# Layer 1's second convolution as a two-phase filter along the columns

## The chip, the cores and the metric

The kernel runs on one core of a Trainium2 chip. The time is the device time of one execution in microseconds. A core has TensorE (PE) for matmuls, with its weight loads shown apart as PEld, VectorE (DVE), ScalarE (ACT), GpSimd (POOL) and SyncE (SP); each has a queue of its own. SP and POOL also start the DMAs of this kernel.

## The reference, cut to what matters

An input of 16 images x 16 channels x 256 x 256 in float32 passes a spectral layer (layer 0) and then layer 1, the one that the change touches:

```python
def _L1_conv_ref(x, W1, b1, Wred, bred, Wspan, bspan, W2, b2, Weca):
    ...
    f = mish(conv2d(xs, W1, b1))
    top, bot = (f[:, :, :H2], f[:, :, H2:])
    ker = conv2d(jax.nn.relu(conv2d(bot, Wred, bred)), Wspan, bspan)
    ...
    top_inv = (patches * ker[:, None]).sum(axis=2)
    ...
    shuffled = shuffled.reshape(B, 4 * C, H, W)
    out = mish(conv2d(shuffled, W2, b2))
    pooled = out.mean(axis=(2, 3))
    ...
    gate = jax.nn.sigmoid(Weca[0] * yp[:, :-2] + Weca[1] * yp[:, 1:-1] + Weca[2] * yp[:, 2:])
    return x * gate[:, :, None, None]
```

The second convolution has 64 input channels, 16 output channels and 3 x 3 taps. Only the mean of its Mish over an image is used. So each output pixel has to be computed, but none is stored.

## The kernel before

The program has four stages: three for layer 0 (`layer0_forward`, `layer0_mix`, `layer0_back`), which end at about 3620 us of the profile, and `layer1` after them. Layer 1 works on one image after the other. An image is cut into nine units (`blocks`): eight of 32 rows x 8 channels, and a ninth with what is left, which has half the work.

A unit passes through these pieces, all methods of `Unit`:

- `lower`: two pairs of matmuls (first convolution of the lower half of the image, names "c", L1027) and four Mish on ScalarE into `bot` (L1046).
- `reduce`: four small matmuls ("pr", L1054), two Relu on ScalarE into `r` (L1063), and the stores of `bot` into the DRAM buffer `cf` (`store_bot`, L1147), issued by GpSimd.
- `upper(0)` and `upper(1)`: a pair of matmuls each (again "c", L1027), and eight Mish each on ScalarE into `wide` (L1075), 32 partitions at a time.
- `spread`: eight copies on GpSimd inside `wide` (L1087, L1088), two for each of four features.
- `involution(0)` to `involution(3)`: two matmuls each ("pd", L1095), and for each of them three VectorE operations (L1103, L1106) into `top`. After the last, `store_top` (L1117, L1124, L1129) writes `top` to `cf`, with GpSimd issuing four or five DMAs, and 16 for a ninth unit.

The second convolution of an image follows one image behind, in eight steps, one for each of the first eight units of the next image. `conv2_rows` loads 17 row pairs of `cf` into one of two buffers `rows2`, on SP, one step ahead. In such a row pair 128 partitions hold 2 rows x 64 channels, and the 256 columns stand in two halves: the odd columns first, then the even ones, with a column of zeros at either end. `conv2` then computes the two column phases one after the other (`q`). Each phase is three column shifts x two row blocks x four groups of 32 output columns of TensorE. The four groups write four quarters of one PSUM bank (`ps2`, one buffer). ScalarE applies Mish to the bank and sums it (L1178).

[...]two buffers of two banks for "c" (`ps1`), three banks for "pd" and "pr" (`psd`), and one for `c2ps` (`ps2`).

When an image's second convolution is done, `gate` computes the 16 gate values in the ninth step and then works on the output in four parts: one in the ninth step, and one in each of the next three. A part is eight scalings on GpSimd (L1216) and two DMAs that it issues (L1225). The loads for the parts (L1193) are in SP's queue.

The order of all these pieces on TensorE, ScalarE, VectorE and GpSimd is written out by hand (`manual_schedule`): an engine takes its instructions in the order in which the loop issues them. A step of the loop (`now` is the current unit, `nxt` the one after it):

```python
            if nxt:
                nxt.lower()
            if now:
                now.involution(0)
            next(second, None)
            ...
            next(last, None)
            next(second, None)
            if now:
                now.involution(3)
```

Between these stand, in order, `nxt.reduce()`, `now.involution(1)`, `nxt.upper(0)`, `now.involution(2)`, `nxt.upper(1)` and `nxt.spread()`. `second` is the step of `conv2`, `last` the gate.

Of the kernel before, what the change touches and what calls it, by code (L numbers as in the profile page):

```python
# [10 lines left out]
F32 = mybir.dt.float32  # L11
I32 = mybir.dt.int32
AF = mybir.ActivationFunctionType
ALU = mybir.AluOpType
# [7 lines left out]
P = 128  # L22
# [34 lines left out]
def load(nc, pool, src, shape, name):  # L57
    t = pool.tile(shape, F32, tag=name, name=name)
    nc.sync.dma_start(out=t, in_=src)
    return t  # L60
# [870 lines left out]
def layer1(ctx, tc, d, zn, cf, mr, nb):  # L931
# [7 lines left out]
    nc = tc.nc  # L939
    H = N // 2  # L940
    wp = ctx.enter_context(tc.tile_pool(name="l1w", bufs=1))
    zp = ctx.enter_context(tc.tile_pool(name="l1z", bufs=4))
    fp = ctx.enter_context(tc.tile_pool(name="l1f", bufs=2))
    rp = ctx.enter_context(tc.tile_pool(name="l1r", bufs=3))
# [3 lines left out]
    psd = ctx.enter_context(tc.tile_pool(name="psd", bufs=3, space=PSUM))  # L948
    ps2 = ctx.enter_context(tc.tile_pool(name="ps2", bufs=1, space=PSUM))
# [6 lines left out]
    wr = load(nc, wp, d["wr"], [P, 32], "wr")  # L956
    dw = load(nc, wp, d["dw"], [P, P], "dw")
    dwt = load(nc, wp, d["dwt"], [P, P], "dwt")
    c2 = load(nc, wp, d["c2"], [P, 2, 3, 32], "c2")
    pm = load(nc, wp, d["pm"], [P, 3, C], "pm")  # L960
    weca = wp.tile([P, 3], F32, name="weca")
    nc.sync.dma_start(out=weca, in_=d["weca"].to_broadcast([P, 3]))
# [8 lines left out]
    b2 = load(nc, wp, d["b2"], [P, 1], "b2")  # L971
# [20 lines left out]
    for t in rows2:  # L992
        for x in (0, N + 1):
            nc.gpsimd.memset(t[:, :, x : x + 1], 0.0)

    def load_rows(b, half, j, h):

        z = zp.tile([P, 8, N + 2], F32, tag="z", name="z")
        flat = z.rearrange("p c x -> p (c x)")
        row = C * (N + 2)  # L1000
        if j < 4:

            m = 8 * (N + 2) - 2
            src = zn[b, H * half + 30 * j, 8 * h, 0:1]
            for dx in range(3):
                win = bass.AP(src.tensor, src.offset + dx, [[row, 32], [1, m]])
                nc.sync.dma_start(out=flat[32 * dx : 32 * dx + 32, :m], in_=win)
            for i in range(2):
                win = bass.AP(src.tensor, src.offset + (32 + i) * row, [[1, 3], [1, m]])
                nc.sync.dma_start(out=flat[96 + 3 * i : 99 + 3 * i, :m], in_=win)  # L1010
            return z
        m = 4 * (N + 2) - 2
        src = zn[b, H * half + 120, 0, 0:1]
        for dx in range(3):
            for c in range(4):
                p = 40 * dx + 10 * c
                win = bass.AP(src.tensor, src.offset + dx + 4 * (N + 2) * c, [[row, 10], [1, m]])
                nc.sync.dma_start(out=flat[p : p + 10, :m], in_=win)
        return z
# [132 lines left out]
    def conv2_rows(b, s):  # L1152
        t = rows2[(8 * b + s) % 2]
        flat = cf[b % 4].rearrange("(t y) f c x -> (y f c) t x", y=2)
        nc.sync.dma_start(out=t[:, :, 1 : N + 1], in_=flat[:, 16 * s : 16 * s + 17])

    def conv2(b, s, acc):


        t = rows2[(8 * b + s) % 2]  # L1160

        begin = ((H + 1, 1, H + 2), (0, H + 1, 1))
        for q in range(2):
            ps = ps2.tile([P, 4, H], F32, tag="c2", name="c2ps")
            for blk in range(2):
                for dx in range(3):
                    x = begin[q][dx]
                    for j in range(4):
                        nc.tensor.matmul(  # L1169
                            ps[32 * j : 32 * j + 32],  # L1170
                            lhsT=c2[:, blk, dx, :],
                            rhs=t[:, 4 * j + blk : 4 * j + blk + 4, x : x + H],
                            start=(blk, dx) == (0, 0),
                            stop=(blk, dx) == (1, 2),
                        )
            e = rp.tile([P, 4, H], F32, tag="e2", name="e2", bufs=2)
            k = 2 * s + q
            nc.scalar.activation(e, ps, AF.Mish, bias=b2, accum_out=acc[:, k : k + 1])  # L1178
            yield

    def gate(b, acc):

# [52 lines left out]
    def begin_unit(i):  # L1235
        if i < len(order):
            b, s = order[i]
            units[i] = Unit(b, i, *blocks[s])

    E = mybir.EngineType  # L1240
    with tc.manual_schedule(engines={E.PE, E.Activation, E.DVE, E.Pool}):
        begin_unit(0)
        begin_unit(1)
        u = units[0]
        u.lower()
        u.reduce()
        u.upper(0)
        u.upper(1)
        u.spread()
        acc, last = None, iter(())  # L1250
        for i in range(9 * nb + 12):
            b, s = divmod(i, 9)
            now, nxt = units.pop(i, None), units.get(i + 1)
            begin_unit(i + 2)
            second = iter(())
            if s == 8 and b < nb:
                conv2_rows(b, 0)
            if s == 8 and b and b <= nb:
                last = gate(b - 1, acc)
                next(last)  # L1260
            if s < 8 and b and b <= nb:
                if s == 0:
                    acc = sm.tile([P, 16], F32, tag="acc", name="acc")
                if s < 7:
                    conv2_rows(b - 1, s + 1)
                second = conv2(b - 1, s, acc)
# [6 lines that stand above are left out]
                nxt.reduce()  # L1273
            if s == 8:
                next(last, None)
            if now:
                now.involution(1)
            if nxt:
                nxt.upper(0)
            if now:  # L1280
                now.involution(2)
            if s == 8:
                next(last, None)
            if nxt:
                nxt.upper(1)
                nxt.spread()
            next(last, None)
            next(second, None)
            if now:
                now.involution(3)  # L1290

# [156 lines left out]
@with_exitstack  # L1450
def forward(ctx, tc, d):
    nb = d["x"].shape[0]
    dram = ctx.enter_context(tc.tile_pool(name="dram", bufs=1, space=DRAM))
    keep = ctx.enter_context(tc.tile_pool(name="keep", bufs=1))
    al = dram.tile([NF, 2, 64, nb, N], F32, name="al")
    bd = dram.tile([nb, P, P], F32, name="bd")
    hd = dram.tile([2, 2, 64, nb, C, N], F32, name="hd")
    tabs = (
        dram.tile([P, 2, C, N], F32, name="td"),
        dram.tile([NF, P, 384], F32, name="avd"),  # L1460
        dram.tile([P, 2, C, N], F32, name="ed"),
    )
    zn = dram.tile([nb, N + 2, C, N + 2], F32, name="zn")
    cf = dram.tile([4, N + 2, 4, C, N], F32, name="cf")
    mr = keep.tile([P, nb, G, 2], F32, name="mr")
    layer0_forward(tc, d, al, bd, tabs)
    layer0_mix(tc, d, al, hd, tabs)
    layer0_back(tc, d, hd, bd, zn, mr, tabs[2])
    layer1(tc, d, zn, cf, mr, nb)
# [25 lines left out]
```

## Time and profile before

| What | Value |
|---|---|
| Median of 3 runs | 7388.45 us (7382.54 to 7390.2) |
| Profiled execution | 7392.98 us |
| Its span | 7391.2 us |
| Mean granted TensorE clock | 0.968 |
| c2ps matmuls (L1169) | 12288, busy 1395.3 us |
| c matmuls (L1027), full units | 2048, busy 1014.2 us |
| pd matmuls (L1095), full units | 2048, busy 1012.5 us |
| Mish into wide (L1075) | 2176, busy 1477.4 us, 679 ns each |
| Copies in wide (L1087, L1088), full units | 1024, 1035 and 1041 ns each |
| Mish of c2ps (L1178) | 256, 687 ns each, then 193 ns for the sum |
| Scalings of the gate (L1216) | 512, 555 ns each |

A float32 matmul is two instructions in the trace, so that 128 steps x 2 phases x 24 matmuls make 12288 rows. The four column groups of c2ps run side by side: the duration of one row (about 600 ns) is not what it takes of TensorE's time. "Busy" counts overlapping rows once. The chain of waits follows the work that ended last backwards; where it stays on one engine, this engine is the bound there. In the timeline, an arrow names what ended the idle time before a row.

### The profile page before, as it was taken

What the parts mean: (1) busy time and instruction counts of PE and PEld (TensorE: products, weight loads), DVE (VectorE), ACT (ScalarE), POOL (GpSimd) and SP (SyncE); (2) the same over time, 40 slices, a digit from 0 to 9 for tenths busy, and PEclk for the clock granted to TensorE, in tenths of its full rate; (3) what the DMA queues carried; (4) which work ended last, traced back from release to release, by engine and by line L of the source; (5) the groups of instructions that cost most, each with busy time, mean ns of one, the idle gap of its engine ahead of it and who ended that gap; (6) DMA issues with size and microseconds to landing.
All of it is one profiled execution on the core that took longest, in us unless ns stands there. A gap on an engine that the chain in (4) does not pass through costs nothing.

```text
span 7391.2 us, 147380 instructions
## 1 busy us (share of the span) xinstructions
PE 6831.1 (92%) x57640; PEld 3890.3 (53%) x57640; DVE 4961.8 (67%) x9441; ACT 3806.5 (51%) x5915; POOL 3475.6 (47%) x4636
## 2 busy tenths in 40 slices
PE   7889999799999999899789999999999999999996
PEld 5778888566666666677423333333333333333332
DVE  8999975366666666788676656665666666666662
ACT  2223333366666666222366656666666666656662
POOL 2334444322222222566554655555665565655554
PEclk9899999899999999999889999999999999999999
DMA  3444444333333332899767888888888888888886
GB/s 99 111 117 119 118 124 117 109 95 97 98 98 98 98 98 83 305 326 326 249 181 221 259 242 253 252 258 254 253 253 251 256 249 267 256 247 251 256 265 205
DMA packets 716089, 1443.59 MB, mean 195 GB/s; under 512 B 98954, under 2 KB 525254, under 8 KB 673638
## 3 DMA queue, kind: packets, MB, share of 16 engines
q1 hardware_dynamic: 567206, 959.76, 43.4%
q0 software_dynamic: 148192, 474.40, 20.6%
q8 instruction: 460, 7.54, 0.4%
q14 instruction: 231, 1.89, 0.1%
HBM read 877.12 MB, written 556.47 MB: 194 GB/s over the span
## 4 chain that ended last, share of the span: by engine, by line
PE 64%; DVE 7%; ACT 4%; issue 3%; DMA 2%; POOL 0%; SPq 0%; DVEq 0%; ACTq 0%; POOLq 0%
PE c2ps L1169 17%; PE c L1027 12%; PE pd L1095 12%; PE ph L698 5%; PE ps L641 5%; PE pg L663 4%; ACT wide L1075 3%; DVE alb L600 2%; PE pr L1054 2%; PE py L858 2%; PE py L859 2%; PE pt L679 1%; DVE zb L890 1%; DVE st L875 1%; DMA rows<-cf 1%
## 5 line engine op out<-in xcount | busy, mean ns | idle before, releaser
L1075 ACT ACTIVATE wide<-c,b 32x512 f32<-32x512 f32 x2176 | 1477.4, 679 | 354.6 <-PE c L1027 302.8
L1103 DVE TENSOR_TENSOR t<-pd,r 64x512 f32<-64x512 f32 x1088 | 744.3, 684 | 1295.9 <-PE pd L1095 1270.3
L1106 DVE TENSOR_TENSOR top<-pd,t 32x512 f32<-32x512 f32 x2176 | 1504.2, 691 | 52.6
L1169 PE MATMUL c2ps<-rows,c 128*32 128x512 f32 x12288 | 1395.3, 601 | 26.6 <-ACT e L1178 13.7
L1087 POOL COPY wide<-wide 32x1031 f32<-32x1031 f32 (+1 forms) x576 | 568.9, 988 | 1239.0 <-ACT wide L1075 1211.7
L1027 PE MATMUL c<-z,w 102*128 102x512 f32 x2048 | 1014.2, 628 | 138.5 <-ACT wide L1075 115.4
L1095 PE MATMUL pd<-wide,dw 128*128 128x512 f32 x2048 | 1012.5, 616 | 6.4 <-ACT r L1063 2.5
L1169 PEld LDWEIGHTS c2ps<-rows,c 128*32 128x32 f32 x12288 | 393.0, 109 | 993.6 <-issue 885.3
L718 POOL DMA_DIRECT2D hd<-h x512 | 323.5, 639 | 1227.6 <-DVE h L711 1203.5
L1027 PEld LDWEIGHTS c<-z,w 102*128 102x128 f32 x2048 | 401.2, 198 | 675.9 <-issue 486.0
L1095 PEld LDWEIGHTS pd<-wide,dw 128*128 128x128 f32 x2048 | 376.8, 194 | 614.3 <-issue 449.0
L1178 ACT ACTIVATE e<-c2ps,b 128x512 f32<-128x512 f32 x256 | 175.9, 687 | 845.6 <-PE c2ps L1169 842.9
L1088 POOL COPY wide<-wide 32x1031 f32<-32x1031 f32 (+1 forms) x576 | 572.2, 993 | 35.8
L313 PE MATMUL px<-wxn,u 128*64 128x256 f32 x4224 | 557.8, 385 | 2.2 <-ACT o L320 2.1
L641 PE MATMUL ps<-tt,lt 128*64 128x256 f32 x4224 | 495.5, 384 | 38.9 <-DVE lt L627 35.9
L698 PE MATMUL ph<-ix,yt 64*128 64x256 f32 x4128 | 502.5, 391 | 5.4 <-issue 4.7
L313 PEld LDWEIGHTS px<-wxn,u 128*64 128x64 f32 x4224 | 400.7, 136 | 127.0 <-ACT o L320 5.1
L698 PEld LDWEIGHTS ph<-ix,yt 64*128 64x128 f32 x4128 | 392.7, 190 | 91.7 <-issue 44.6
L1046 ACT ACTIVATE bot<-c,b 128x512 f32<-128x512 f32 x544 | 344.1, 684 | 175.7 <-PE c L1027 168.2
L207 PE MATMUL pu<-fy,eo 128*128 128x128 f32 x2048 | 425.5, 291 | 6.0 <-DVE u L224 4.4
L320 ACT ACTIVATE o<-px,rsc 128x512 f32<-128x512 f32 (+1 forms) x272 | 186.0, 686 | 472.2 <-PE px L313 441.1
L871 POOL TENSOR_TENSOR x<-x,o 128x512 f32<-128x512 f32 x256 | 324.0, 1266 | 216.7 <-DVE o L870 215.3
(203 smaller groups left out, 10818.5 us busy)
## 6 DMA issues: line engine op xcount, KB each, us to landing
rows<-cf SPq DMA_DIRECT2D x128, 2176.0 KB
z<-zn SPq DMA_DIRECT2D x768, 257.8 KB
cf<-top POOLq DMA_DIRECT2D x512, 240.0 KB, 7.1
cf<-bot POOLq DMA_DIRECT2D x96, 840.0 KB, 11.6
alc<-al SPq DMA_DIRECT2D x264, 256.0 KB
zn<-zb SPq DMA_DIRECT2D x128, 516.0 KB
o<-zn SPq DMA_DIRECT2D x128, 516.0 KB
z<-in_x SPq DMA_DIRECT2D x64, 1024.0 KB
```

The costliest lines, as they stand in the source:

```text
L207: nc.tensor.matmul(pu[:, xh, e].rearrange("p v m -> p (v m)"), lhsT=lhs, rhs=fy[:, e], start=True, stop=True,)
L313: nc.tensor.matmul(ps[64 * k : 64 * k + 64, :, h], lhsT=u[:, h, part, g0 + j + k].rearrange("p f c -> p (f c)"), rhs=wxn[:, h, part], star ...
L641: nc.tensor.matmul(ps[64 * h : 64 * h + 64, v], lhsT=lt[:, h, k, 1 - v : 3 - v].rearrange("p l f c -> p (l f c)"), rhs=tt[:, h, k], start= ...
L698: nc.tensor.matmul(ph[q][:, e], lhsT=yt[lanes, i].rearrange("p t k -> p (t k)"), rhs=ix[lanes, i], start=n == 0, stop=n == 3,)
L1027: nc.tensor.matmul(ps[:, a], lhsT=w, rhs=z[:k, c : c + 2, 0:N], start=True, stop=True)
L1075: nc.scalar.activation(self.feat[64 - 32 * q : 96 - 32 * q, f, self.groups[g], :H], ps[q][32 * f : 32 * f + 32], AF.Mish, bias=b1[0][32 * ...
L1087: nc.gpsimd.tensor_copy(flat[0:32, f, 1:m], flat[64:96, f, 0 : m - 1])
L1088: nc.gpsimd.tensor_copy(flat[96:128, f, 0 : m - 1], flat[32:64, f, 1:m])
L1095: nc.tensor.matmul(ps, lhsT=dwt if self.tail else dw, rhs=self.feat[:, f, cs, :H], start=True, stop=True,)
L1103: nc.vector.tensor_tensor(t[64:128], ps[:64], self.r[:, cs], ALU.mult)
L1106: nc.vector.tensor_tensor(self.top[32 * f : 32 * f + 32, cs, q], ps[lanes], t[lanes], ALU.add)
L1169: nc.tensor.matmul(ps[32 * j : 32 * j + 32], lhsT=c2[:, blk, dx, :], rhs=t[:, 4 * j + blk : 4 * j + blk + 4, x : x + H], start=(blk, dx) = ...
```

## The change

The odd and even output columns are no longer computed apart. With the even input columns e and the odd ones o, and the three taps w0, w1, w2 of a row, one phase of the output is w1 on one set of columns plus w0 and w2 on the other. The changed `conv2` makes three pieces of this:

1. w1 on the even columns (one product, 16 of TensorE's instructions), which ScalarE copies to an SBUF tile `mid` with one more column of zeros.
2. w0 and w2 on the odd columns (two products). VectorE adds the copy to this twice: at the same column for `even`, which is one phase of the output, and shifted by a column for `both`.
3. w0 and w1 + w2 on `pair`, the sum of the neighbouring odd and even columns (two products). VectorE subtracts `both` from it, which leaves the other phase, `odd`.

The sum `pair` is one GpSimd addition over 17 x 129 columns at the start of a step; the tile has one buffer. The sum of the weights, `c2s`, is made once. Mish with the sum over columns is applied to `even` and `odd`, in place in SBUF. The generator yields four times in place of two, and the loop takes it on at two more places. In the last image, whose second convolution runs without units beside it, the second piece takes its bank from `psd`.

```diff
     c2 = load(nc, wp, d["c2"], [P, 2, 3, 32], "c2")
+    c2s = wp.tile([P, 2, 32], F32, name="c2s")
+    nc.vector.tensor_tensor(c2s, c2[:, :, 1], c2[:, :, 2], ALU.add)
...
+    pair = wp.tile([P, 17, H + 1], F32, name="pair")
+    mid = [wp.tile([P, 4, H + 1], F32, name=f"mid{i}") for i in range(2)]
+    for t in mid:
+        nc.gpsimd.memset(t[:, :, H : H + 1], 0.0)
...
         t = rows2[(8 * b + s) % 2]
-
-        begin = ((H + 1, 1, H + 2), (0, H + 1, 1))
-        for q in range(2):
-            ps = ps2.tile([P, 4, H], F32, tag="c2", name="c2ps")
-            for blk in range(2):
-                for dx in range(3):
-                    x = begin[q][dx]
+        nc.gpsimd.tensor_tensor(pair, t[:, :, H + 1 :], t[:, :, : H + 1], ALU.add)
+
+        def products(terms, n=0):
+            pool, tag = (psd, "d") if n % 2 and b == nb - 1 else (ps2, "c2")
+            ps = pool.tile([P, 4, H], F32, tag=tag, name="c2ps")
+            for i, (w, src, x) in enumerate(terms):
+                for blk in range(2):
                     for j in range(4):
                         nc.tensor.matmul(
                             ps[32 * j : 32 * j + 32],
-                            lhsT=c2[:, blk, dx, :],
-                            rhs=t[:, 4 * j + blk : 4 * j + blk + 4, x : x + H],
-                            start=(blk, dx) == (0, 0),
-                            stop=(blk, dx) == (1, 2),
+                            lhsT=w[:, blk],
+                            rhs=src[:, 4 * j + blk : 4 * j + blk + 4, x : x + H],
+                            start=(i, blk) == (0, 0),
+                            stop=(i, blk) == (len(terms) - 1, 1),
                         )
-            e = rp.tile([P, 4, H], F32, tag="e2", name="e2", bufs=2)
+            return ps
+
+        def pooled(y, q):
             k = 2 * s + q
-            nc.scalar.activation(e, ps, AF.Mish, bias=b2, accum_out=acc[:, k : k + 1])
-            yield
+            nc.scalar.activation(y, y, AF.Mish, bias=b2, accum_out=acc[:, k : k + 1])
+
+        a = mid[s % 2]
+        nc.scalar.copy(a[:, :, :H], products([(c2[:, :, 1], t, H + 1)]))
+        yield
+        ps = products([(c2[:, :, 0], t, 0), (c2[:, :, 2], t, 1)], 1)
+        even = rp.tile([P, 4, H], F32, tag="even", name="even", bufs=2)
+        nc.vector.tensor_tensor(even, ps, a[:, :, :H], ALU.add)
+        both = rp.tile([P, 4, H], F32, tag="both", name="both", bufs=2)
+        nc.vector.tensor_tensor(both, ps, a[:, :, 1:], ALU.add)
+        yield
+        pooled(even, 0)
+        ps = products([(c2[:, :, 0], pair, 0), (c2s, pair, 1)])
+        odd = rp.tile([P, 4, H], F32, tag="odd", name="odd", bufs=2)
+        nc.vector.tensor_tensor(odd, ps, both, ALU.subtract)
+        yield
+        pooled(odd, 1)
+        yield
...
             if now:
                 now.involution(1)
+            next(second, None)
             if nxt:
                 nxt.upper(0)
...
             next(second, None)
             if now:
                 now.involution(3)
+            next(second, None)
```

## The prediction

> **What bounds the kernel now.** I read the page's busy shares first, then the windows of 200 us, to leave layer 0 (up to about 3620 us) out of it, then the chain of waits in one stretch of layer 1, and last the timeline by engine in that stretch. The page says that TensorE is busy for 92% of the span; a window in the middle of layer 1 says more (columns: PE, PEld, DVE, ACT, POOL busy us, then granted clock, DMA share, GB/s).
>
> ```profile
> PE 6831.1 (92%) x57640; PEld 3890.3 (53%) x57640; DVE 4961.8 (67%) x9441; ACT 3806.5 (51%) x5915; POOL 3475.6 (47%) x4636
> ...
> 5600.00:5800.00 200.00, 193.36 (x976) 69.47 (x975) 125.34 (x187) 124.47 (x197) 121.62 (x172) 0.97 0.85 260
> ```
>
> TensorE is busy 97% there, and the other three engines 61 to 63%. The chain of waits of one step (start, us, what) is TensorE alone:
>
> ```profile
> 5730.26 1.91 PE pd L1095 x4
> 5732.17 3.44 PE c L1027 x8
> 5735.61 1.72 PE pd L1095 x4
> 5737.32 5.37 PE c2ps L1169 x45
> 5742.70 0.86 PE pr L1054 x8
> 5743.55 1.91 PE pd L1095 x4
> 5745.47 1.72 PE c L1027 x4
> 5747.19 1.72 PE pd L1095 x4
> 5748.90 1.72 PE c L1027 x4
> 5750.62 5.33 PE c2ps L1169 x43
> ```
>
> The ten pieces run without a hole, 25.7 us a step, and the second convolution (c2ps) is two of them, 10.74 us. A half is 48 instructions (3 column shifts x 2 blocks x 4 column groups, each matmul twice in the trace), four at a time: 5.37/12 = 0.4475 us for four. A pd piece after c2ps or pr takes 1.91 us, elsewhere 1.72: each change from 32 to 128 columns costs 0.19. But the holes are near. The timeline of the ninth step, which has no second convolution, and of the step after it:
>
> ```profile
> 5669.02 11.24 ACT L1075 ACTIVATE wide<-c,b 32x512 f32<-32x512 f32 x16
> ...
> 5674.68 3.78 PE L1027 MATMUL c<-z,w 102*128 102x512 f32 x4 [3.60 <-ACT wide L1075]
> ...
> 5690.94 3.54 POOL L1124 DMA_DIRECT2D cf<-top  x7
> ...
> 5696.06 3.98 POOL L1124 DMA_DIRECT2D cf<-top  x8 [1.57 <-DMA out_dram<-o]
> ...
> 5699.06 5.44 PE L1169 MATMUL c2ps<-rows,c 128*32 128x512 f32 x48
> ...
> 5702.05 0.50 POOL L1124 DMA_DIRECT2D cf<-top  x1 [2.01 <-DMA cf<-top]
> ```
>
> Three things are to be seen. ScalarE needs 11.24 us for the 16 "wide" pieces of a unit, and where TensorE's work between is shorter, TensorE waits (3.60 us) for a "c1" buffer. GpSimd is still issuing the ninth step's stores when TensorE begins the second half of the first convolution step. And the c piece after the wait took 3.46 us in the chain, twice its 1.72.
>
> **What the Trainium skill says.** "GPSIMD Engine Reference", 3.1 Elementwise, gives 4497 ns for a tensor_tensor add of 2048 fp32 a partition. The trace agrees:
>
> ```profile
> L871 POOL TENSOR_TENSOR x<-x,o 128x512 f32<-128x512 f32 x256 | 324.0, 1266 | 216.7 <-DVE o L870 215.3
> L194 POOL TENSOR_TENSOR eo<-z 128x1024 f32<-128x1024 f32 x64 | 155.1, 2423 | 332.4 <-PE pv L214 310.7 <-DMA z<-in_x 15.3 <-issue 6.3
> ```
>
> "TensorE: Matmul & The Clock Gate", Part 1, says that the array drops to half clock after an idle window of about 3.4 us and needs a busy one to come back; the doubled c piece agrees. The same page (32x32 sub-arrays, engine queue depths) has GpSimd, VectorE and ScalarE take instructions strictly in order; GpSimd's rows above come in program order.
>
> **The change, part by part.** A conv2 step has 5 products (a product is 2 blocks x 4 groups) in place of 6: 80 instructions for 96, so 4 fours less, 4 x 0.4475 = 1.79 us. In three pieces in place of two there is one more change of columns: +0.19. TensorE gains 1.60 us a step, 12.8 us a batch of 8 steps. That is the whole gain.
>
> *VectorE* gets three 128x512 additions a step (even, both, odd), 0.69 us each by the rows of 684 to 691 ns: +2.1 on 17.3 us of a 24 us step. They stand in its queue behind the tops of an involution; by the in-order count "even" and "both" end at about 1.6 us after their product, and the PSUM bank is wanted 5.3 us after it. Cover enough; if gone, 0.7 us each. *ScalarE* gets the copy of the first product (nearest rows: 585 to 687 ns), at a place where it stood idle for 5.9 us waiting for c2ps; the bank is wanted 2.8 us after the product, the copy ends 0.9 us after. The two Mish with accumulation remain, 0.88 us each, from SBUF. c2s and the memsets run once. I cost these at nothing.
>
> *ScalarE's wide pieces lose cover.* From the end of upper(0) to the second matmul pair of the next lower(), TensorE had 1.72 + 1.72 + 5.37 + 1.91 + 1.72 = 12.4 us of work; ScalarE needs 0.26 to start and 11.24. Now the c2ps piece between is 3.58 (the other 3.58 went ahead of upper(0)), so 10.65 us: that matmul waits about 0.9 us. Behind it stands all of TensorE. The loop ScalarE-TensorE is then 25.1 us a step, a gain of 0.6 rather than 1.6, wherever nothing else has stopped TensorE in that step. Bounds: 0 (ScalarE might start earlier) and 0.9.
>
> *GpSimd's sum "pair"* is 17 x 129 = 2193 elements: from 1266 and 2423 ns, 2.26 ns an element, 5.07 us; the page's price scales to 4.8; 6 us if the padded rows cost more. It is queued behind the former step's stores, and ahead of store_bot and spread; the third product waits for it, and all of TensorE behind that. In steps 4 to 7 GpSimd is idle for 14 us before its copies (7 in step 3), and the sum ends at U + 23.1 where the product comes at U + 28.5 (both worked out as for step 2 below): hidden; without that cover it would be 5.07 us a step. In steps 0 to 3 a gate part (6.65 us) is in the queue too. Step 0: the 16 stores end at 5702.55 us, the sum at 5707.7; TensorE comes to the third product at 5685.83 (end of involution(0)) + 1.79 + 0.86 + 1.91 + 3.58 + 1.91 + 1.72 + 1.72 = 5699.3. Wait: 8.4 us. Over twelve batches with a gate the stores end 1.0 to 5.5 us after the old second half's start, 2.8 on the mean, so the mean wait is 7.8. After such an idle time the clock halves: +2.6 us (bounds 1.7 and 3.4, a half of 3.4 to 6.8 us). Step 1 just fits. Step 2: upper(0)'s end U, copies from U + 7.3 for 8.7, gate 6.65, stores 2.65, sum 5.07 = U + 30.4, wanted at U + 28.5: 2.1 with the semaphore. Step 3: 0.3.
>
> *Sum of a batch with gate:* -12.8, +7.8 +2.6 +2.4 for the sum, +4.6 for ScalarE's cover in the five steps that no longer wait (0.9, 0.6, 0.9, 0.9, 0.9 and 0.4 into the tail): +4.6 us. Fourteen of them: +64. The first batch has no gate: -12.8 + 1.1 + 5.5 = -6. The last batch runs without units: 5.44 + 0.96 us a half, 104 us in all. There steps 0 to 3 follow GpSimd's queue (16 stores to 7269.9, then sum and gate part in turn to 7311, third product 7315 against 7303), and steps 4 to 7 take 10.0 us for 12.75: +1, with the halved clock +4. Total +62. The profiled execution took 7392.98 us (span 7391.2), so 7455; it lies 4.5 above the median, so against the median **7450**.
>
> **Rivals.**
> 1. *Faster: the sum is not late in step 0.* For it: GpSimd's 16 stores wait 3.6 us of their 11.6 for DMAs, which may fall otherwise; in one batch they end only 1.0 us late. Against: the order is fixed and even then the sum is 6 us late. From stores that end 5 us ahead of the old second half it decides: the 7.8 and 2.6 go, -5.8 a batch x 14 - 6 = about **7305**; without ScalarE's wait too, down to 7240.
> 2. *No difference: ScalarE's wait does not appear.* For it: before, TensorE had 1 us to spare there, and buffers might come free earlier. A batch is then 12.8 - 12.8 = 0; with -11 for the first and +4 at the end about **7381**.
> 3. *Much slower: GpSimd's delay reaches further.* The gate's loads stand in SP's queue ahead of the next unit's; where a part leaves 5 to 10 us later, SP holds the z loads. Against: they are issued a step ahead. Three us more in each of four steps, 14 x 4 x 3 = 168: **7618**.
> That the change doesn't save the products is excluded by the count.
>
> **How the numbers follow.** The forecast 0.58 (own range 7405 to 7500, from 4.8 to 6 us for the sum and the bounds of clock and cover), rival 1 0.24, rival 2 0.12, rival 3 0.06. Under 0.2% (15 us) a measurement can't tell from no change. Faster 0.24, same 0.12, slower 0.64. The range 7290 to 7510 takes in about half of rival 1 and leaves rival 3 out.
>
> **What would show it.** c2ps matmuls 10240 and about 1163 us; the new GpSimd addition at 5 us, 128 times; c2ps waiting for GpSimd about 8 us once a batch, and the next pieces at double length; c waiting for wide some 0.9 us in steps 4 to 7. If the addition takes under 3 us, or GpSimd reaches it before TensorE in step 0, the forecast is wrong; if c never waits for wide, by 4.6 us a batch.

## The result and the profile after

The changed kernel took 7437.15 us (median of 4 runs, 7434.99 to 7446.27), the kernel before 7385.49 us beside it: a ratio of 1.0076, 95% interval 1.0058 to 1.0093. So the change costs some 52 us, though TensorE does less. The page of the changed kernel, parts 1 and 5 (columns as before):

```profile
PE 6701.7 (90%) x55592; PEld 3766.3 (51%) x55592; DVE 5217.3 (70%) x9826; ACT 3870.4 (52%) x6043; POOL 4095.1 (55%) x4766
...
L1083 ACT ACTIVATE wide<-c,b 32x512 f32<-32x512 f32 x2176 | 1476.9, 679 | 830.2 <-PE c L1035 778.4
...
L1171 POOL TENSOR_TENSOR pair<-rows 128x2193 f32<-128x2193 f32 x128 | 624.1, 4876 | 26.7 <-PE c2ps L1179 13.6
```

TensorE has 2048 instructions and 129 us of busy time less than before. The products did go; GpSimd has 620 us more, which is the new sum, 128 times 4.88 us. What TensorE waited for inside layer 1 (4000 to 7000 us) says where the gain went. The columns are us in total, times, longest:

```profile
PE c L1035 <- ACT wide L1083: 113.9, 77, 3.6
PE c2ps L1179 <- POOL pair L1171: 109.8, 39, 9.6
```

The same view of the kernel before has, for the first of them:

```profile
PE c L1027 <- ACT wide L1075: 74.1, 26, 3.6
```

The second line did not exist before. The 26 waits of the first all stood in ninth steps; now there are 77, so 51 short ones are new. Two stretches show both. First the start of a batch, GpSimd's own timeline and then TensorE's:

```profile
5704.74 5.03 POOL L1132 DMA_DIRECT2D cf<-top  x10
...
5715.89 1.15 POOL L1132 DMA_DIRECT2D cf<-top  x2 [2.89 <-DMA cf<-top]
5717.06 4.83 POOL L1171 TENSOR_TENSOR pair<-rows 128x2193 f32<-128x2193 f32 x1
5721.82 1.09 POOL L1155 DMA_DIRECT2D cf<-bot  x2
```

```profile
5712.86 1.88 PE L1035 MATMUL c<-z,w 102*128 102x512 f32 x4
5721.94 3.21 PE L1179 MATMUL c2ps<-pair,c 128*32 128x512 f32 x16 [7.20 <-POOL pair L1171]
5724.98 1.90 PE L1179 MATMUL c2ps<-pair,c2s 128*32 128x512 f32 x16
```

GpSimd gets to the sum only when the last of the ninth step's 16 stores is issued. TensorE stands still for 7.20 us with nothing else in its queue that it may take, and begins again at a lower clock: the first 16 instructions take 3.21 us, the next 16, of the same shape, 1.90. The granted clock of these two stretches is 0.56 and 1.00 (columns as in the prediction's window, the clock behind the five engines):

```profile
5721.94:5724.98 3.04, 3.04 (x17) 0.76 (x21) 0.00 (x0) 1.50 (x3) 2.94 (x4) 0.56 0.60 114
5724.98:5726.80 1.82, 1.82 (x20) 0.37 (x12) 0.00 (x0) 0.00 (x0) 1.70 (x3) 1.00 1.06 407
```

Over the 14 batches with a gate beside units the wait is 5.9 to 9.6 us, 7.2 on the mean.

Then a step in the second half of a batch, in the chain of waits:

```profile
5833.70 1.72 PE pd L1103 x4
5835.41 1.89 PE c2ps L1179 x16
5837.31 0.86 PE pr L1062 x8
5838.16 1.99 PE pd L1103 x4
5840.16 3.62 PE c2ps L1179 x29
5843.78 1.93 PE c L1035 x4
5845.80 0.68 ACT wide L1083
...
5856.35 0.69 ACT wide L1083
5857.09 1.99 PE c L1035 x4
5859.07 1.29 PE pd L1103 x3
```

Where the chain before was TensorE alone, it now leaves TensorE after upper(0), runs through ScalarE's wide pieces for 11.2 us and comes back. The step takes 25.37 us (5833.70 to 5859.07) for 25.7 before: of the 1.6 us that the count of matmuls promised, 0.3 is left.

### The profile page after: what moved, and what is told of

Its sections match the earlier page's. It is cut to its first block, busy times and chain, and to the rows that moved or that the text cites. A ratio compares the mean times of both kernels' runs of the same rounds, so it can differ in the third digit from the quotient of the medians.

```text
span 7433.4 us, 143886 instructions
## 1 busy us (share of the span) xinstructions
PE 6701.7 (90%) x55592; PEld 3766.3 (51%) x55592; DVE 5217.3 (70%) x9826; ACT 3870.4 (52%) x6043; POOL 4095.1 (55%) x4766
## 4 chain that ended last, share of the span: by engine, by line
PE 23%; ACT 11%; POOL 9%; issue 3%; DMA 3%; DVE 2%; SPq 0%; POOLq 0%; ACTq 0%; DVEq 0%
ACT wide L1083 10%; PE c2ps L1179 9%; PE c L1035 6%; PE pd L1103 6%; POOL pair L1171 3%; POOL o L1244 3%; DMA cf<-top 1%; PE pr L1062 1%; POOL wide L1096 1%; DVE top L1114 1%; POOL wide L1095 1%; POOL cf L1132 1%; DVE t L1111 1%; DMA z<-zn 1%; DMA out_dram<-o 1%
## 5 line engine op out<-in xcount | busy, mean ns | idle before, releaser
L1035 PE MATMUL c<-z,w 102*128 102x512 f32 x2048 | 1040.1, 635 | 185.3 <-ACT wide L1083 163.6
L1103 PE MATMUL pd<-wide,dw 128*128 128x512 f32 x2048 | 1027.9, 623 | 13.0 <-DVE top L1114 8.1
L1035 PEld LDWEIGHTS c<-z,w 102*128 102x128 f32 x2048 | 385.0, 197 | 784.6 <-issue 490.5
L1179 PE MATMUL c2ps<-rows,c 128*32 128x512 f32 x6144 | 723.7, 603 | 9.4 <-DMA rows<-cf 5.3
L1171 POOL TENSOR_TENSOR pair<-rows 128x2193 f32<-128x2193 f32 x128 | 624.1, 4876 | 26.7 <-PE c2ps L1179 13.6
L1179 PEld LDWEIGHTS c2ps<-rows,c 128*32 128x32 f32 x6144 | 176.5, 109 | 519.6 <-issue 429.4
L329 POOL DMA_DIRECT2D al<-o x544 | 322.9, 606 | 204.7 <-ACT o L320 192.4
```

Source lines behind the costliest of these rows:

```text
L1035: nc.tensor.matmul(ps[:, a], lhsT=w, rhs=z[:k, c : c + 2, 0:N], start=True, stop=True)
L1103: nc.tensor.matmul(ps, lhsT=dwt if self.tail else dw, rhs=self.feat[:, f, cs, :H], start=True, stop=True,)
L1171: nc.gpsimd.tensor_tensor(pair, t[:, :, H + 1 :], t[:, :, : H + 1], ALU.add)
L1179: nc.tensor.matmul(ps[32 * j : 32 * j + 32], lhsT=w[:, blk], rhs=src[:, 4 * j + blk : 4 * j + blk + 4, x : x + H], start=(i, blk) == (0, 0 ...
```

## The experiments

Each ratio is to the kernel before, timed beside it on the same chip.

**1. The third piece without the sum**

```diff
-        nc.gpsimd.tensor_tensor(pair, t[:, :, H + 1 :], t[:, :, : H + 1], ALU.add)
...
-        ps = products([(c2[:, :, 0], pair, 0), (c2s, pair, 1)])
+        ps = products([(c2[:, :, 0], t, 0), (c2s, t, 1)])
```

> The GpSimd sum is left out: the third piece takes its two products from the loaded rows in place of the sum, with the same number of matmuls, so the values of one column phase are not those of the convolution. Theory (the sum is late and stops TensorE, and ScalarE's shorter cover takes most of the rest): no c2ps wait on GpSimd; c waits for wide by 0.75 us in nearly every step, steps of 25.4 us; per batch 3.6 - 9.7 (the waits and the halved clock) + 1.8 (ScalarE waits that come back) = -4.3 us against before; about 7310 us, ratio to before 0.990 (0.986 to 0.994). Rival A (the sum is innocent: smaller pieces, the VectorE and ScalarE additions or the clock cost the time): as the changed kernel, ratio 1.006 to 1.008. Rival B (all of the count returns once the sum is gone, ScalarE's cover does not matter): 0.974.

Measured: 7324.49 us, ratio 0.9915 (0.9901 to 0.993). TensorE's waits in its profile, 4000 to 7000 us:

```profile
PE c L1034 <- ACT wide L1082: 138.7, 107, 3.6
```

No wait for the sum is left, and in a batch that was read step by step the short waits for ScalarE (0.70 to 0.72 us) stand in all six steps from the second to the seventh. The sum made the change a loss (rival A falls); but without it only 0.85% of the 2.6% that rival B expects comes out, so something else takes most of it; these waits point to ScalarE's cover, which run 3 tries.

**2. The sum alone, in the kernel before**

```diff
+    pair = wp.tile([P, 17, H + 1], F32, name="pair")
...
+        nc.gpsimd.tensor_tensor(pair, t[:, :, H + 1 :], t[:, :, : H + 1], ALU.add)
         begin = ((H + 1, 1, H + 2), (0, H + 1, 1))
```

> The kernel before with the GpSimd sum added at the same place in GpSimd's queue; nothing reads it. Theory (the sum costs because TensorE waits for it, not because GpSimd is busier): no wait of c2ps; only GpSimd's copies of the first convolution step come some 5 us later, of which 3.3 us are slack: +1.6 us a batch, ratio 1.001 to 1.005. Rival C (the load on GpSimd by itself stops TensorE, through copies, stores and buffers): 8 us a batch, ratio 1.015 to 1.02.

Measured: 7408.17 us, ratio 1.0027 (1.0018 to 1.0036). The same sum, 627 us of GpSimd's time, costs 19 us when no product waits for the result. The expected wait for late copies is there, a row of TensorE's timeline at the start of a batch:

```profile
6157.10 3.48 PE L1097 MATMUL pd<-wide,dw 128*128 128x512 f32 x4 [2.47 <-POOL wide L1090]
```

But over 4000 to 7000 us there are only 7 such waits, 7.0 us together, and the kernel before has 9.4 us of waits for rows in that stretch that this trace has not. Most of the loss stands at the end, where the last image runs without units: from the last 3.60 us wait of a ninth step to the end the trace has 376.99 us for 358.37. From 7030 us on TensorE waits for rows of the second convolution, and two loads of rows, in SP's queue, wait for the sum, which reads the buffer that they fill:

```profile
PE c2ps L1172 <- DMA rows<-cf: 16.7, 3, 9.3
SPq L1157 <- POOL pair L1164: 10.1, 2, 9.2
```

Before, TensorE waited there for rows twice, 3.4 us together. How much of the 16.7 us comes from these two loads was not tried. Rival C, 1.015 or more, falls.

**3. The second and third piece later**

```diff
                 now.involution(1)
-            next(second, None)
...
                 now.involution(3)
             next(second, None)
+            next(second, None)
```

The second piece thereby falls behind upper(1) and spread, and the third behind involution(3).

> The changed kernel with the second piece after upper(1) and spread, and the third after involution(3): all of c2ps but the first product stands between upper(0) and the next lower. Theory: ScalarE's cover is 16 us for 11.5, so no c waits for wide in the first eight steps, which take 24.2 us; the sum has 1.9 us more at step 0, so a wait of about 5.3 us and the halved clock stay there, and steps 1 to 3 have none: -5.5 us a batch, about 7305 us, ratio 0.989 (0.985 to 0.992). Rival D (the waits of c for wide are a shadow, another wait takes their place): ratio 1.003 to 1.008.

Measured: 7319.92 us, ratio 0.9909 (0.9892 to 0.9926). TensorE's waits, 4000 to 7000 us:

```profile
PE c L1035 <- ACT wide L1083: 86.4, 28, 3.6
PE c2ps L1179 <- POOL pair L1171: 64.5, 15, 8.1
```

The 28 waits for ScalarE are two for each of the ninth steps, as before the change; the short ones are gone and nothing takes their place (rival D falls). The waits for the sum are down from 39 to 15: twelve stand at the first step of a batch (4.0 to 8.1 us), three elsewhere (under 1 us each). In the two batches that seem to have none, the same instruction waits 3.8 us; the view puts these two down to VectorE, whose operation, in the one that was read, ended at the same moment as the sum.

**4. The gate parts one step later**

```diff
                 nxt.spread()
-            next(last, None)
+            if s < 8 or b == nb:
+                next(last, None)
```

> The changed kernel with the four gate parts one step later each (steps 0 to 3 in place of 8 and 0 to 2), which takes 6.65 us out of GpSimd's queue ahead of the first sum. Theory: the wait of step 0 falls from 7.2 us to 0.5 and the halved clock goes; 0.75 us of ScalarE's wait comes back: -3.4 us a batch, about 7332 us, ratio 0.993 (0.990 to 0.996). Rival A (the sum is innocent): no change from the changed kernel, 1.006 to 1.008. Rival E (the tail's stores wait for their DMAs longer and keep the sum as late): 1.004 to 1.007.

Measured: 7325.44 us, ratio 0.9913 (0.9898 to 0.9928). TensorE's waits, 4000 to 7000 us:

```profile
PE c L1035 <- ACT wide L1083: 106.2, 73, 3.6
PE c2ps L1179 <- POOL pair L1171: 44.0, 62, 4.5
```

The sum of a batch's first step is now 0.6 to 1.9 us late in twelve of the fourteen batches (4.5 us in one, not late in one), in place of about 7, and those of the next steps mostly by 0.2 to 0.8 us: more waits, but short ones. No matmul, sum or addition was changed here. What this run wins back was lost by the order of GpSimd's queue, not by the amount of its work.

**5. Both moves together**

> The two moves of e3 and e4 together: products later and gate parts one step later. Theory: the first sum ends within 0.3 us of where the third piece wants it, no c waits for wide in the first eight steps, so what the count of matmuls promises is left: -12.8 us a batch with 0.5 to 1.5 us of small waits, 15 batches, the last image 5 us longer: about 7205 us, ratio 0.975 (0.973 to 0.980). Rival F (GpSimd or VectorE becomes the bound once TensorE is faster: copies, psd banks, loads): ratio 0.983 to 0.988, little better than either move alone.

Measured: 7208.43 us, ratio 0.976 (0.9745 to 0.9775). Waits of TensorE, 4000 to 7000 us, and the chain of one step:

```profile
PE c L1035 <- ACT wide L1083: 79.9, 28, 3.6
...
PE c2ps L1179 <- POOL pair L1171: 4.6, 4, 2.2
```

```profile
5629.72 1.88 PE c2ps L1179 x14
5631.60 0.86 PE pr L1062 x7
5632.46 2.00 PE pd L1103 x4
5634.46 1.72 PE c L1035 x4
5636.18 1.72 PE pd L1103 x4
5637.90 1.72 PE c L1035 x4
5639.62 3.62 PE c2ps L1179 x29
5643.24 1.91 PE pd L1103 x4
5645.15 3.57 PE c2ps L1179 x32
5648.72 3.63 PE c L1035 x8
5652.36 1.72 PE pd L1103 x4
```

The chain is TensorE alone again, and a step takes 24.35 us (5629.72 to 5654.07, the next step's first product). This kernel beats both: 2.4% less than before, 3.1% less than the changed kernel. The two moves add up: alone they gain 117 and 112 us on the changed kernel's 7437 us, together 229.

**6. A control: the gate parts later in the kernel before**

> A control: the kernel before with the four gate parts one step later each, and nothing else. Theory (this move is worth something only where TensorE waits for GpSimd): as before, ratio 0.998 to 1.002. Rival G (the gate parts cost time in the ninth step anyway, so that the gain of the combined kernel is partly this): 0.990 to 0.995.

Measured: 7389.37 us, ratio 1.0001 (0.9992 to 1.001). The edit of run 4 is worth nothing where TensorE does not wait for GpSimd, so rival G falls: run 5's gain is not that edit's own, apart from the sum.

**7. The sum a step earlier, with two buffers**

```diff
+    pairs = [wp.tile([P, 17, H + 1], F32, name=f"pair{i}") for i in range(2)]
...
                 nxt.spread()
+            if s == 8 and b < nb:
+                pair_sum(b, 0)
+            elif s < 7 and b and b <= nb:
+                pair_sum(b - 1, s + 1)
             next(last, None)
```

The sum at the start of a step is gone, and the third piece reads `pairs[s % 2]`.

> The changed kernel with two buffers for the sum, and the sum issued a step ahead, right after spread and ahead of the gate part and the stores. Theory (GpSimd's whole queue from the ninth step to the second is too long, not only the place of the sum in it): c2ps never waits for GpSimd beside units, but the copies of the first step end some 2 us late and pd waits for them once a batch; ScalarE's waits come back in all steps; ratio 0.994 to 0.998, so worse than without the sum (0.9915). Rival H (only the place of the sum in the queue matters): as without the sum, 0.990 to 0.993.

Measured: 7471.46 us, ratio 1.011 (1.0095 to 1.0125), worse than the changed kernel. Both expectations missed. In TensorE's timeline no wait for the sum is left beside units, and the late copies are there as expected:

```profile
6208.90 3.11 PE L1103 MATMUL pd<-wide,dw 128*128 128x512 f32 x4 [2.38 <-POOL wide L1096]
```

But a wait that no expectation had stands at the fourth step, 11 times for 57.4 us in 4000 to 7000 us (and TensorE's waits there for VectorE's tops are 25.6 us in 35, for 6.1 us in 13 in the changed kernel):

```profile
6268.18 3.32 PE L1183 MATMUL c2ps<-rows,c 128*32 128x512 f32 x16 [4.54 <-DMA rows<-cf]
```

The waits of SP's queue name a likely cause, first in this kernel, then in the changed one:

```profile
SPq L1225 <- DMA out_dram<-o: 551.7, 52, 21.8
```

```profile
SPq L1221 <- DMA out_dram<-o: 456.3, 52, 17.1
```

The gate's loads (L1225 here) can't start before an earlier part has left its buffer. With the sums ahead of the gate parts, GpSimd issues those stores later, SP stands up to 21.8 us at the gate's load, and the next units' loads and the rows of the second convolution are behind it in the same queue. In the batch of the row above, SP stands at the gate's load until 6227.51 us and issues the fourth step's rows at 6246.83, 21.4 us ahead of the start of the product that waits for them. Over the batches with a gate this lead of the fourth step's rows is 18 to 23 us; in the changed kernel, where no such wait stands beside units, it is 29 to 33. The sums of the waits in SP's queue do not show the cause by themselves: run 3 has 575.9 us of them (longest 17.3), more than run 7, with a lead of 25 to 29 us and no late rows beside units. The longer wait, the shorter lead and the late rows are measured; that the first makes the others was not tried by itself.

## Why the prediction was right

Forecast: slower, 7450 us; measured 7437.15. By its own steps (those of a batch counted from 0, as there):

- *The count.* 1.60 us a step. Run 5, the nearest to no other limit, shows 25.7 - 24.35 = 1.35: the first product's piece takes 1.88 us where the sum had 1.79, the pd piece after pr 2.00 for 1.91, and the second piece 3.62 for 3.58. Over eight steps the gain was taken 2.0 us too high.
- *ScalarE's cover.* A wait of 0.9 us and a step of 25.1 were forecast (its own terms, 25.7 - 1.6 + 0.9, give 25.0); the trace shows 0.75 us and 25.37. Run 3 shows that the cover is the cause, and that it was the order of the pieces, not ScalarE's added work: its copies and Mish are all still there in run 3. The size was right too: the 0.75 counts from the modelled end of the piece before, but from start to start the two c pieces in the rows below stand 2.63 us apart, where without a wait it is 1.72. TensorE goes on 0.91 us later. The next piece then comes 1.83 us on in place of 1.72, and the rest of the 25.37 is what the count lacks:

```profile
5752.98 1.88 PE L1035 MATMUL c<-z,w 102*128 102x512 f32 x4
5755.61 1.99 PE L1035 MATMUL c<-z,w 102*128 102x512 f32 x4 [0.75 <-ACT wide L1083]
5757.44 1.88 PE L1103 MATMUL pd<-wide,dw 128*128 128x512 f32 x4
```

- *The sum.* 5.07 us forecast, 4.88 measured. The wait at a batch's first step: 7.8 forecast, 7.2 measured. Steps 2 and 3: 2.1 and 0.3 forecast, 0.78 and 0.18 in most batches. The 0.78 adds nothing to the loss: step 2 takes 25.38 us like the steps that wait for ScalarE, so this wait only stands in the place of theirs. For steps 1 to 7 the sum's 2.4 and the cover's 4.6 were forecast, 7.0 together; against run 5, five steps are longer by 1.02 and one, ahead of the ninth, by 0.6: 5.7. The two runs that touch only GpSimd's side (1 and 4) confirm the sum as what makes the loss.
- *The halved clock.* +2.6 us forecast, bounds 1.7 and 3.4. The 32 instructions after the first step's wait take 4.86 to 6.52 us where they take 3.57 without one: over the fourteen batches 1.3 to 3.0 us more, 2.0 on the mean.
- *Nothing for VectorE and ScalarE's additions.* VectorE has 256 us more and ScalarE 64. Run 5 contains all of it and is TensorE alone in the chain, so this holds, but for one wait of 0.47 us a batch for a bank that VectorE frees late, in the changed kernel's eighth step.
- *The sum of a batch.* +4.6 us forecast. From the ninth step's wait of one batch to that of the next (thirteen intervals with a gate) the trace of before has 227.18 us on the mean and that of after 230.82: +3.64. Two of before's intervals are longer than the rest, with waits for rows; by the medians, 226.46 and 230.56, it is +4.1. The first batch: -6 forecast, -4.1 measured. The rest, the fourteenth batch and the last image: 6.2 us more, which leaves 2.6 for the image where 4 was forecast, though its first wait for the sum is 16.5 us where the forecast's 7315 against 7303 has 12.

The mechanism is the forecast's: which waits, and in which steps. That the sum came so close is in part luck. The count's gain was taken 2.0 us a batch too high, the first wait and its clock 1.2 us too high, the later steps 1.3 us too high; these errors, of both signs, lead from 4.6 to the 4.1 of the medians.

Up to the first of these marks the profiled execution of after was 7.2 us ahead (3851.04 for 3858.25 us), almost all of it in stages that the change leaves alone. So the spans differ by 42.2 us, and what lies behind that mark by 49.4. The medians differ by 51.7.

Of the rivals, the first and second fall by the waits of 5.9 us or more for the sum and the 51 new waits for ScalarE. The third (SP's queue held by the gate's loads) did not appear in the changed kernel beside units: no wait for rows in 4000 to 7000 us (5.3 us in the last image). It probably did in run 7.

## What to carry to other kernels

When work is taken from the bounding engine, ask of every other in-order queue not how busy it is on the mean, but what stands in it at the worst step of the period and when the new consumer wants the result: 5 us more on an engine that was 61% busy stopped the bound one for 7. Ask also which work of the bounding engine was cover for somebody else's chain, and where its remaining pieces should stand so that they still are. The same saving was worth -0.8% or +2.4% only by the order of issue.

## What the runs showed of the hardware that was not expected

- A wait of only 1.92 us was once followed by half of TensorE's clock: in run 4, with 1.00 granted up to its end, 0.50 was granted for the next 3.42 us (from 5431.95 us). A wait of 2.98 us in the last image of the changed kernel (up to 7358.21 us) was followed by 1.00. In these traces the length of one wait does not tell what the clock does after it; the forecast went by about 3.4 us.
- After a wait of only 0.75 us, with 1.00 granted, the next piece starts 1.83 us after the one that waited, where it is 1.72 without a wait.
- Mish on a 128x512 tile takes 687 ns from PSUM (before) and 709 to 722 ns in place in SBUF (after).
